# A graph network's edge pass on one core: other choice of column copies, a buffer of its own for the sums, and one-hot weights by whole-group operations

## The chip, the core and the metric

The kernel runs on one NeuronCore of a Trainium2 chip. Its engines are PE (TensorE: matmuls, with weight loads shown as PEld), DVE (VectorE), ACT (ScalarE), POOL (GpSimd) and SP (SyncE, which only issues transfers). The metric is the device time of one execution in microseconds (us), the median of several runs. Each engine has its own queue of instructions, works them off in order, and waits on semaphores for what other engines or transfers have to deliver.

## The reference

One layer of message passing over 12500 nodes (64 features) and 412500 directed edges, which are sorted by receiver and carry 32 features each. Cut to what matters:

```python
h = relu(layernorm(x))                                              # 12500 x 64
m = concat([h[senders], h[receivers], edge_features], -1)           # 412500 x 160
messages = silu(m @ W1 + b1) @ W2 + b2
att = softmax(silu(m @ Wa1 + ba1) @ Wa2 + ba2, axis=0)              # over ALL edges
aggregated = segment_sum(messages * att, receivers, 12500)
out = x + silu(concat([h, aggregated], -1) @ Wu1 + bu1) @ Wu2 + bu2
```

## The kernel before, in words

Edges are cut into 3224 tiles of 128 and those into 403 *groups* of 8 tiles (`K`). The input of both hidden layers is split: `h[senders] @ W` and `h[receivers] @ W` are computed once per node, not per edge.

**Node phase.** In chunks of up to 14 blocks of 128 nodes: layer norm, transposes into `hT` (128 partitions: even blocks in the lower 64, odd blocks in the upper 64), and from it two tables in DRAM of 128 columns a node: `ts_d` for senders (written from SP's queue) and `tr_d` for receivers (ACT's queue). A copy of `hT` goes to DRAM as `hT_d`.

**The loop over groups** (`one_pass`) emits its work in an order written out by hand; `pin` keeps it so in each engine's queue.

- `load(g + 2)`: POOL issues one indirect gather per tile (L533), 128 rows of `ts_d` by sender into the buffer `gs` (a pool of 7). Every fourth group, edge features and receivers' numbers come by SP. SP brings the window of receiver rows (L554). DVE builds the receivers' one-hot columns `eo` (L558), and PE adds window rows and edge features into `pe` (L562).
- `begin(g)`: DVE adds `pe` to the gathered rows, in place in `gs` (L573), ACT takes the tanh (L576).
- `end(g)`: DVE forms the messages (L586) and the attention logits (L592, L594, L597); a batch of 4 groups ends with its maximum (L609 to L616).
- `sum_up(done)`, some five groups behind: `weigh` updates the running maximum and takes exponentials; `by_node` makes the weights `wt`, the softmax weight times a one-hot of the receiver in a window of 40 nodes, by eight DVE operations, one per tile (L640), and PE sums the messages with them into `sp` (L646); `out_of` copies `sp` to `ss` on ACT (L652); `project` multiplies by W2 (L657); `put` adds to `sums` (L671, L675) and notes in `stand` which maximum the sums stand on (L678), for 64 partitions each.
- In a *chosen* group (127 of them) the eighth tile isn't gathered. ACT copies the senders' columns out of `hT` one by one (128 copies, L504, column numbers in registers), in bursts spread over three groups (`SLOTS`, two bursts a group). The column numbers are computed for each group on DVE (`places`, L487 to L493) from 128 copies of the sender list (`numbers`); another operation (L567) zeroes the half of the 128 partitions that isn't the sender's, and PE multiplies by `stack`, the weights laid over both halves.
- Between these, pieces of the last stage's inputs are made ahead (L348, L357, L389).

**The tail**, after the last group, makes 13 output tiles: `factor` (ACT, L830: exponential of the standing maximum less the last one), `first` (DVE L838, POOL L843), `silu` (ACT L848, DVE L849), `second` (PE L856), `rest` (DVE L862, transfers out). The loop of the tail issues, for tile number t, `first(t)`, `factor(t + 1)`, `silu(t - 1)`, `second(t - 1)`, `rest(t - 2)`.

`general` is another path for inputs whose receivers leave wide gaps; it isn't executed here.

Of the kernel before, what the change touches and what calls it, by code (L numbers as in the profile page):

```python
# [45 lines left out]
I32 = mybir.dt.int32  # L46
# [27 lines left out]
EVERY = 3  # L74
PHASE = 1
SLOTS = (((0, 24), (24, 24)), ((48, 24), (72, 12)), ((84, 24), (108, 20)))
# [4 lines left out]
BIG = 3.0e38  # L81


PARTS = [("pair", 4 * C), ("we", C), ("bias", C), ("wu2h", 2 * D), ("wa2", U), ("bu2", D), ("w_bu", U),
         ("w2b", U), ("wu1a", U), ("wu2", D), ("ba2", 1), ("w_bup", 2 * U), ("bu1", 1)]
# [5 lines left out]
def gnn_kernel(ctx: ExitStack, tc: tile.TileContext, n_edges, x, src, src_row, dst, dst_row, first, edge,  # L91
# [14 lines left out]
    hT_d = dram.tile([2 * D, NB // 2, P], F32, name="hT_d")  # L106
# [19 lines left out]
    w_bu = part["w_bu"][:D + 1]  # L126
# [29 lines left out]
    hT = const.tile([2 * D, NB // 2, P], F32, name="hT")  # L156
# [5 lines left out]
    gather = ctx.enter_context(tc.tile_pool(name="gather", bufs=7))  # L162


    with tc.tile_pool(name="node1", bufs=1) as node1, \
# [7 lines left out]
        for c, n in chunks:  # L173
            xc = node.tile([P, CB, D], F32, name="xc", bufs=min(len(chunks), 8))[:, :n, :]
# [138 lines left out]
        pin(nc.scalar.dma_start(hT_d, hT))  # L313
# [6 lines left out]


def node_bias(tc, b, v, work, ps):

    nc = tc.nc
    NB, w_bu = v["NB"], v["w_bu"]
    n = min(4, NB - b)
    hb = work.tile([D + 1, 4, P], F32, name="hb")
    nc.vector.memset(hb[D:, :, :], 1.0)
    for r in range(2):
        nc.sync.dma_start(hb[:D, r:n:2, :], v["hT_d"][r * D:(r + 1) * D, b // 2:(b + n) // 2, :])  # L330
    pb = ps.tile([P, 4, P], F32, name="mt")
    nc.tensor.matmul(pb[:U, :n, :], w_bu, hb[:, :n, :], start=True, stop=True)
    return pb[:U, :n, :]
# [60 lines left out]
def one_pass(tc, n_edges, v):  # L394
# [17 lines left out]
    with ExitStack() as ctx:  # L412
# [5 lines left out]
        stand = keep.tile([P, NH + 2 * W], F32, name="stand")  # L418
# [15 lines left out]
        nc.vector.memset(start[:, 1:2], BIG)  # L434
# [5 lines left out]
        hT = v["hT"].rearrange("d b p -> d (b p)")  # L440
        stack = keep.tile([2 * D, C], F32, name="stack")
        nc.vector.tensor_tensor(stack, v["w_pair"][:, 0, :C], v["w_pair"][:, 0, C:], ALU.add)
        half = keep.tile([P, 1], F32, name="half")
        nc.vector.memset(half[:D], 0.0)
        nc.vector.memset(half[D:], 1.0)
# [10 lines left out]
        with tc.tile_pool(name="work2", bufs=2) as work2, \  # L456
# [3 lines left out]
            pes, gss, lgs, ps_, psums, sps, pps, ees, mts, nums, cols = ({} for _ in range(11))  # L460
# [11 lines left out]
            chosen = {g for g in range(8, NG - 12) if g % EVERY == PHASE}  # L472

            def numbers(g):
                if g in chosen:
                    e = (g * K + K - 1) * EP
                    n = nums[g] = small.tile([P, EP], I32, name="num", bufs=2)
                    nc.sync.dma_start(n, bass.AP(tensor=v["src_row"].tensor,
                                                 offset=v["src_row"][:, e:].offset, ap=[[0, P], [1, EP]]))

            def places(g):
                if g not in chosen:
                    return
                n = nums[g]
                near = small.tile([1, EP], F32, name="near", bufs=1)
                to = small.tile([1, EP], I32, name="to", bufs=2)
                pin(nc.vector.tensor_scalar(to, n[0:1], 1, None, op0=ALU.logical_shift_right))  # L487
                m = NB // 2
                pin(nc.vector.tensor_scalar(near, to, 1.0 / m, 0.5 / m - 0.5, op0=ALU.mult, op1=ALU.add))
                pin(nc.vector.tensor_scalar(near, near, ROUND, None, op0=ALU.add))  # L490
                pin(nc.vector.tensor_scalar(near, near, ROUND, float(1 - m * P), op0=ALU.subtract, op1=ALU.mult))
                pin(nc.vector.scalar_tensor_tensor(to, to, float(P), near, op0=ALU.mult, op1=ALU.add))
                pin(nc.vector.tensor_scalar(n, n, 1, None, op0=ALU.bitwise_and))  # L493
                cols[g] = small.tile([P, EP], F32, name="cols", bufs=2), to

            def columns(g, first, n):
                if g not in chosen:
                    return
                to, at = cols[g]
                _, regs = nc.values_load_multi_w_load_instructions(  # L500
                    at[0:1, first:first + n], engines=[ENG.Activation], min_val=0, max_val=NP // 2 - 1,
                    skip_runtime_bounds_check_because=WHY)
                for i in range(n):
                    pin(nc.scalar.copy(to[:, first + i:first + i + 1], hT[:, bass.ds(regs[i], 1)]))  # L504
# [19 lines left out]
            def load(g):  # L524
# [40 lines left out]
                if g in chosen:  # L565
                    to, _ = cols[g]
                    pin(nc.vector.scalar_tensor_tensor(to, nums[g], half, to, op0=ALU.is_equal, op1=ALU.mult))  # L567
                    pin(nc.tensor.matmul(pe[:, K - 1, :], to, stack, start=False, stop=True))

            def begin(g):  # L570

                n = K - (g in chosen)
                pin(nc.vector.tensor_tensor(gss[g][:, :n, :], pes[g][:, :n, :], gss[g][:, :n, :], ALU.add))  # L573
                if n < K:
                    pin(nc.vector.tensor_copy(gss[g][:, n, :], pes[g][:, n, :]))
                pin(nc.scalar.activation(pes[g], gss[g], AF.Tanh))  # L576

            def end(g, then=None):
# [4 lines left out]
                gs, th = gss.pop(g), pes.pop(g)  # L583
# [50 lines left out]
            def by_node(g):  # L634
# [4 lines left out]
                for j in range(K):  # L639
                    pin(nc.vector.tensor_scalar(wt[:, j, :], iota_w[:EP, j // H, :],  # L640
                                                dloc[:, g * K + j:g * K + j + 1],
                                                p[:, k + j:k + j + 1],
                                                op0=ALU.is_equal, op1=ALU.mult))
# [5 lines left out]
            def out_of(g):  # L649
                sp = sps[g]  # L650
                ss = sps[g] = work2.tile([S1, W], F32, name="ss")
                pin(nc.scalar.copy(ss, sp))  # L652
# [7 lines left out]
            def put(g, part=None):  # L660
# [5 lines left out]
                for h, at in enumerate((at_lo, at_hi)):  # L666
                    rows, cols = slice(h * U, (h + 1) * U), bass.ds(at[g], W)
                    if part != "stand":
                        pp = pps[g]
                        if g == starts[s]:  # L670
                            pin(nc.vector.scalar_tensor_tensor(sums[rows, cols], sums[rows, cols],  # L671
                                                               scale[rows, s:s + 1], pp[rows],
                                                               op0=ALU.mult, op1=ALU.add))
                        else:
                            pin(nc.vector.tensor_tensor(sums[rows, cols], sums[rows, cols], pp[rows],  # L675
                                                        ALU.add))
# [11 lines left out]
            def inputs(t):  # L688

                n = P // 2 * NC  # L690
                if t < 8:
                    i = (t // 4 + (NG - 1) // NQ + 1) % 2
                    bs[t], xs[t] = eos[i][:, t % 4 * n:(t % 4 + 1) * n], hT[:, t * n:(t + 1) * n]
# [40 lines left out]

            for g in range(AHEAD):
                load(g)
            done = 0
            for g in range(NG):
# [9 lines left out]
                if g < 4:  # L748
                    w = -(-(NH + 2 * W) // 4)
                    for k, table in enumerate((sums, stand)):  # L750
                        piece = table[:, g * w:min((g + 1) * w, NH + 2 * W)]
                        pin(nc.scalar.activation(
                            piece, start[:, k:k + 1].to_broadcast([P, piece.shape[1]]), AF.Copy))
# [5 lines left out]
                numbers(g + 7)  # L759
                places(g + 6)  # L760
# [56 lines left out]
            free = [gather.tile([P, K, C], F32, name="gs").rearrange("p k c -> p (k c)") for _ in range(2)]  # L817
            free.append(hT[:, 8 * P // 2 * NC:8 * P // 2 * NC + K * C])
# [6 lines left out]
            def factor(t):  # L825
                n = width(t)
                if t in (1, 2):
                    acts_ps.append(one_ps.tile([P, 4, P], F32, name=(None, "sp", "mt")[t]).rearrange("p k c -> p (k c)"))
                fac = facs[t] = acts_ps[t % 3][:, :P // 2 * n]
                pin(nc.scalar.activation(fac.rearrange("u (p b) -> u p b", b=n),  # L830
                                         fv[:, :, t * NC:t * NC + n], AF.Exp, bias=last, scale=-1.0))
# [59 lines left out]
def general(tc, n_edges, v, dst):  # L891
# [7 lines left out]
    with ExitStack() as ctx:  # L899
# [11 lines left out]
        dst_sb = keep.tile([EP, T], I32, name="dst_g")  # L911
# [14 lines left out]
        with tc.tile_pool(name="bu_g", bufs=2) as work, \  # L926
                tc.tile_pool(name="bu_g_ps", bufs=2, space=PSUM) as bu_ps:
            for b in range(0, NB, 4):
                n = min(4, NB - b)
                bu = work.tile([U, 4, P], F32, name="bu_g")[:, :n, :]  # L930
                nc.scalar.copy(bu, node_bias(tc, b, v, work, bu_ps))
                nc.sync.dma_start(bu_d[:, b:b + n, :], bu)
# [142 lines left out]
def _laid_out(w):  # L1075
# [17 lines left out]
    part["w_bu"][:D + 1] = np.concatenate([w["Wu1"][:D], w["bu1"][None]])  # L1093
# [47 lines left out]
```

## Time and profile before

| | |
|---|---|
| median of 3 runs | 3987.03 us (3986.22 to 3988.06) |
| profiled execution | 3986.92 us, of it 3985.1 in the profile's span |
| busy: DVE / POOL / PE / ACT | 82% / 74% / 59% / 55% of the span |
| gathers (L533) | 3097, mean 947 ns |
| column copies (L504) | 16256 (127 groups x 128) |
| one-hot weights (L640) | 3224 operations, 726.1 us |
| mean clock granted to PE | 0.64 of full speed |

A row of the page's groups reads: line, engine, operation, out<-in, count, then busy us and mean ns of one, then the idle time of the engine just before these instructions and what ended most of it ("<-DMA gs": a transfer into `gs`; "<-issue": nothing the profile shows). A row of the timeline reads: start in us, length, engine, line, operation, and in brackets the idle time before it and who ended it.

### The profile page before, as it was taken

To read this page: it belongs to the slowest core of one execution; us is meant where nothing else is said; L and a number is where in the kernel's file an instruction comes from. 1 tells how busy PE (TensorE), PEld (TensorE's weight loads), DVE (VectorE), ACT (ScalarE), POOL (GpSimd) and SP (SyncE) were. 2 spreads that over 40 slices of the span, in tenths; PEclk is the share of its full clock that TensorE was granted. 3 is DMA by queue.
4 is the path that set the end of the run, shared out by engine and by line. 5 is a ranking of instruction groups with operands and counts; after the bars stand their busy time and mean duration, and the time that the engine had idled before them with its cause. 6 is when DMAs were issued, how large, how long until landed. Compare 5 with 4: busy or idle time off the path is not lost. (4 is left out here: it accounts for less than half of the span.)

```text
span 3985.1 us, 80416 instructions
## 1 busy us (share of the span) xinstructions
PE 2332.9 (59%) x11238; PEld 1888.3 (47%) x11238; DVE 3264.8 (82%) x9553; ACT 2173.0 (55%) x17477; POOL 2950.2 (74%) x3122
## 2 busy tenths in 40 slices
PE   6556566666666555555555555555655555555566
PEld 5444444454444444444444444444544444444455
DVE  6888888888888787888878888887878887878787
ACT  3655555555555555555555555555555555555512
POOL 3777777777777777777777777777777777777774
PEclk8766666666666666666666666666666665666666
DMA  8333343333333333333333333333333333333333
GB/s 287 101 99 99 95 110 92 103 99 102 102 92 95 93 85 93 87 92 88 89 94 84 95 93 86 94 84 94 88 91 94 84 95 87 91 95 84 104 105 85
DMA packets 219778, 391.64 MB, mean 98 GB/s; under 512 B 72209, under 2 KB 146898, under 8 KB 206050
## 3 DMA queue, kind: packets, MB, share of 16 engines
q0 software_dynamic: 99104, 203.16, 19.1%
q1 hardware_dynamic: 118754, 173.60, 16.7%
q10 hardware_dynamic: 1376, 9.67, 0.6%
q14 instruction: 452, 3.70, 0.3%
q8 instruction: 92, 1.51, 0.2%
HBM read 360.42 MB, written 25.72 MB: 97 GB/s over the span
## 5 line engine op out<-in xcount | busy, mean ns | idle before, releaser
L533 POOL DMA_INDIRECT gs<-ts_d,src_sb x3097 | 2933.0, 947 | 992.6 <-issue 854.1
L562 PE MATMUL pe<-wins,eo 128*128 128x256 f32 x3224 | 1465.1, 630 | 925.7 <-DVE eo L558 679.6
L504 ACT COPY cols<-hT 128x1 f32 x16256 | 1605.0, 187 | 717.7 <-issue 714.8
L562 PEld LDWEIGHTS pe<-wins,eo 128*128 128x128 f32 x3224 | 970.9, 318 | 1222.7 <-DVE eo L558 769.0
L576 ACT ACTIVATE pe<-gs 128x1024 f32<-128x1024 f32 x403 | 413.7, 1026 | 928.6 <-DVE gs L573 496.8
L573 DVE TENSOR_TENSOR gs<-pe,gs 128x1024 f32<-128x1024 f32 (+1 forms) x403 | 475.4, 1180 | 393.6 <-DMA gs<-ts_d,src_sb 369.2
L640 DVE TENSOR_SCALAR wt<-iota_w,dloc,p 128x40 f32<-128x40 f32 x3224 | 726.1, 321 | 1.8
L646 PE MATMUL sp<-wt,acts 128*65 128x40 f32 x6448 | 628.8, 268 | 6.3 <-DVE wt L640 3.9
L646 PEld LDWEIGHTS sp<-wt,acts 128*65 128x65 f32 x6448 | 589.9, 183 | 16.2 <-DVE wt L640 9.7
L657 PEld LDWEIGHTS mt<-ss,w2u 65*128 65x128 f32 x806 | 203.0, 279 | 336.2 <-issue 173.9
L657 PE MATMUL mt<-ss,w2u 65*128 65x40 f32 x806 | 181.6, 319 | 242.3 <-DVE gm L623 202.0
L616 PE MATMUL mt<-ident,mx 128*128 128x128 f32 x107 | 47.4, 443 | 445.8 <-DVE sums L675 427.2
L594 DVE TENSOR_TENSOR pe<-pe,w_all 128x512 f32<-128x512 f32 x403 | 281.8, 699 | 13.4
L558 DVE TENSOR_SCALAR eo<-dbs,bj 64x256 f32<-64x256 int32 x806 | 277.9, 375 | 18.2 <-DMA dbs<-in_dst_row_dram 9.0
L592 DVE SCALAR_TENSOR_TENSOR pe<-pe,gs 128x512 f32<-128x512 f32 x403 | 280.3, 696 | 10.5
L586 DVE SCALAR_TENSOR_TENSOR acts<-pe,gs 128x512 f32<-128x512 f32 x403 | 277.2, 688 | 12.4 <-ACT pe L576 3.2
L597 DVE TENSOR_REDUCE lg<-pe 128x8 f32<-128x512 f32 x403 | 277.0, 687 | 10.5
L616 PEld LDWEIGHTS mt<-ident,mx 128*128 128x128 f32 x107 | 19.5, 182 | 456.9 <-issue 455.0
L678 DVE COPY stand<-nmax 64x40 f32 x806 | 161.0, 200 | 3.2
L671 DVE SCALAR_TENSOR_TENSOR sums<-sums,scale,mt 64x40 f32 x214 | 54.2, 253 | 89.2 <-PE mt L657 85.0
L675 DVE TENSOR_TENSOR sums<-sums,mt 64x40 f32 x592 | 111.5, 188 | 4.7 <-PE mt L657 0.6
L357 DVE TENSOR_SCALAR bu<-mt,w_all 64x256 f32<-64x256 f32 (+1 forms) x50 | 23.9, 477 | 88.7 <-PE mt L348 88.3
(124 smaller groups left out, 1062.7 us busy)
## 6 DMA issues: line engine op xcount, KB each, us to landing
eo<-in_edge_dram SPq DMA_DIRECT2D x100, 512.0 KB
dbs<-in_dst_row_dram SPq DMA_DIRECT2D x200, 256.0 KB
gs<-ts_d,src_sb POOLq DMA_INDIRECT x3097
wins<-tr_d SPq DMA_DIRECT2D x806, 32.0 KB
num<-in_src_row_dram SPq DMA_DIRECT2D x127, 64.0 KB
ts_d<-ts SPq DMA_DIRECT2D x5, 896.0 KB
tr_d<-tr ACTq DMA_DIRECT2D x5, 896.0 KB
hT_d<-hT ACTq DMA_DIRECT2D x1, 3136.0 KB
```

The source lines that it names most:

```text
L504: pin(nc.scalar.copy(to[:, first + i:first + i + 1], hT[:, bass.ds(regs[i], 1)]))
L533: nc.gpsimd.indirect_dma_start(out=full[:rows, j, :], out_offset=None, in_=ts_d[:, :], in_offset=bass.IndirectOffsetOnAxis(ap=src_full[:ro ...
L558: pin(nc.vector.tensor_scalar(eo[:WR, e], db[:, e], bj[g // NQ % 2 * WR:(g // NQ % 2 + 1) * WR, g, h:h + 1], None, op0=ALU.is_equal))
L562: pin(nc.tensor.matmul(pe[:, 2 * q:2 * q + 2, :], eo[:, q * EP:(q + 1) * EP], win[:, q // 2, :, :], start=True, stop=q < H - 1 or g not in ...
L573: pin(nc.vector.tensor_tensor(gss[g][:, :n, :], pes[g][:, :n, :], gss[g][:, :n, :], ALU.add))
L576: pin(nc.scalar.activation(pes[g], gss[g], AF.Tanh))
L586: pin(nc.vector.scalar_tensor_tensor(acts[g % ACTS][:, :, 0:U], th[:, :, U:C], 1.0, gs[:, :, U:C], op0=ALU.add, op1=ALU.mult))
L592: pin(nc.vector.scalar_tensor_tensor(att, th[:, :, 0:U], 1.0, gs[:, :, 0:U], op0=ALU.add, op1=ALU.mult))
L594: pin(nc.vector.tensor_tensor(att, att, wa2[:EP, None, :].to_broadcast([EP, K, U]), ALU.mult))
L640: pin(nc.vector.tensor_scalar(wt[:, j, :], iota_w[:EP, j // H, :], dloc[:, g * K + j:g * K + j + 1], p[:, k + j:k + j + 1], op0=ALU.is_equ ...
L646: pin(nc.tensor.matmul(sp, acts[g % ACTS][:, j, :], wt[:, j, :], start=j == 0, stop=j == K - 1))
L657: pin(nc.tensor.matmul(pp, w2u.rearrange("s h u -> s (h u)"), sps.pop(g), start=True, stop=True))
```

## The change

It does five things together.

1. *Another choice of groups.* Chosen are now the groups from 10 to 390 whose number leaves 0 or 3 by five: 153, not 127. A chosen group's 128 copies come in five pieces of 28, 24, 28, 24 and 24, one per half step of the loop.
2. *Lists made once.* The column numbers of all chosen groups are computed at the start by 14 DVE operations and written to DRAM (`list_d`); each chosen group then loads its own 512 bytes (`listed`). The transposed nodes lie in a wider tile, `hS`, whose lower 64 partitions get a copy of the upper half (`upper`, four transfers on SP in the first four steps), so that a column is 64 partitions high, and the zeroing (L567) and `stack` are gone. `hT_d` and its write are gone. The upper 64 partitions of the added part of `hS` now hold `stand`, with 32 partitions per half in place of 64.
3. *A buffer of their own for the sums.* The addition writes to `sm` (2 buffers) and frees the gather's buffer, of which there are 5 in place of 7.
4. *Whole-group weights.* `by_node` has two operations over 128x320 (compare, multiply) in place of eight over 128x40. `out_of` copies on DVE in place of ACT.
5. *The tail.* Because `stand` has fewer partitions, `factor` first spreads its rows by a PE matmul with `pick` into PSUM, and ACT takes the exponential there. Two of the tail's spare buffers are taken from `sm`.

The diff, cut to its core ("..." marks what is left out):

```diff
-EVERY = 3
-PHASE = 1
-SLOTS = (((0, 24), (24, 24)), ((48, 24), (72, 12)), ((84, 24), (108, 20)))
+EVERY = 5
+LEADS = {0: 9, 3: 10}
+SLOTS = ((0, 28), (28, 24), (52, 28), (80, 24), (104, 24))
+FIRST = 10
...
-    hT_d = dram.tile([2 * D, NB // 2, P], F32, name="hT_d")
+    list_d = dram.tile([len(LEADS), P, EP], I32, name="list_d")
...
-    hT = const.tile([2 * D, NB // 2, P], F32, name="hT")
+    hS = const.tile([2 * D, NP + 2 * W], F32, name="hS")
+    hT = hS[:, :NP // 2].rearrange("d (b p) -> d b p", p=P)
...
-    gather = ctx.enter_context(tc.tile_pool(name="gather", bufs=7))
+    gather = ctx.enter_context(tc.tile_pool(name="gather", bufs=5))
...
-        pin(nc.scalar.dma_start(hT_d, hT))
...
-        stand = keep.tile([P, NH + 2 * W], F32, name="stand")
+        stand = v["hS"][D:, NH:]
...
-        stack = keep.tile([2 * D, C], F32, name="stack")
...
+        w_s = v["w_pair"][:D, 0, :C]
+        pick = keep.tile([P, P], F32, name="pick")
+        nc.vector.memset(pick, 0.0)
+        for h in range(2):
+            nc.vector.memset(pick[D + R * h:D + R * h + 1, h * U:(h + 1) * U], 1.0)
...
-            chosen = {g for g in range(8, NG - 12) if g % EVERY == PHASE}
+            chosen = [g for g in range(FIRST, NG - 12) if g % EVERY in LEADS]
+            def column_lists():
...
+                    pin(nc.vector.tensor_scalar(to, num, 1, None, op0=ALU.logical_shift_right))
...
+                    pin(nc.vector.scalar_tensor_tensor(column, num, float(NH), near, op0=ALU.mult, op1=ALU.add))
+                    nc.sync.dma_start(v["list_d"][i, :n, :], column)
+            def upper(k, n):
+                w = -(-NH // n)
+                a, b = k * w, min((k + 1) * w, NH)
+                nc.sync.dma_start(hS[:D, NH + a:NH + b], hS[D:, a:b])
+            def listed(g):
                 if g in chosen:
+                    to = lists[g] = small.tile([1, EP], I32, name="listed", bufs=3)
+                    nc.sync.dma_start(to, v["list_d"][list(LEADS).index(g % EVERY),
+                                                      (g - of_phase[g % EVERY][0]) // EVERY][None, :])
...
-                    pin(nc.scalar.copy(to[:, first + i:first + i + 1], hT[:, bass.ds(regs[i], 1)]))
+                    pin(nc.scalar.copy(cols[g][:, first + i:first + i + 1], hS[:D, bass.ds(regs[i], 1)]))
             def burst(g, k):
-                for i in range(EVERY):
-                    columns(g + 3 + i, *SLOTS[EVERY - 1 - i][k])
+                for c in range(g, g + 7):
+                    if c in chosen and 0 <= 2 * g + k - (2 * c - LEADS[c % EVERY]) < len(SLOTS):
+                        columns(c, *SLOTS[2 * g + k - (2 * c - LEADS[c % EVERY])])
...
-                    pin(nc.vector.scalar_tensor_tensor(to, nums[g], half, to, op0=ALU.is_equal, op1=ALU.mult))
-                    pin(nc.tensor.matmul(pe[:, K - 1, :], to, stack, start=False, stop=True))
+                    pin(nc.tensor.matmul(pe[:, K - 1, :], cols.pop(g), w_s, start=False, stop=True))
             def begin(g):
-                n = K - (g in chosen)
-                pin(nc.vector.tensor_tensor(gss[g][:, :n, :], pes[g][:, :n, :], gss[g][:, :n, :], ALU.add))
+                n, gs = K - (g in chosen), gss.pop(g)
+                sm = sms[g] = work2.tile([EP, K, C], F32, name="sm", bufs=2)
+                pin(nc.vector.tensor_tensor(sm[:, :n, :], pes[g][:, :n, :], gs[:, :n, :], ALU.add))
...
                 wt = work2.tile([EP, K, W], F32, name="wt")
                 p = ps_[batch[g]]
-                for j in range(K):
-                    pin(nc.vector.tensor_scalar(wt[:, j, :], iota_w[:EP, j // H, :],
-                                                dloc[:, g * K + j:g * K + j + 1],
-                                                p[:, k + j:k + j + 1],
-                                                op0=ALU.is_equal, op1=ALU.mult))
+                at = dloc[:, g * K:(g + 1) * K].rearrange("p (h j) -> p h j", h=2)
+                pin(nc.vector.tensor_tensor(wt.rearrange("p (h j) w -> p h j w", h=2),
+                                            iota_w[:EP, :, None, :].to_broadcast([EP, 2, H, W]),
+                                            at[:, :, :, None].to_broadcast([EP, 2, H, W]), ALU.is_equal))
+                pin(nc.vector.tensor_tensor(wt, wt, p[:, k:k + K, None].to_broadcast([EP, K, W]), ALU.mult))
...
-                pin(nc.scalar.copy(ss, sp))
+                pin(nc.vector.tensor_copy(ss, sp))
...
-                        pin(nc.vector.tensor_copy(stand[rows, cols],
-                                                  nmax[rows, s + 1:s + 2].to_broadcast([U, W])))
+                        pin(nc.vector.tensor_copy(stand[h * R:(h + 1) * R, cells],
+                                                  nmax[h * R:(h + 1) * R, s + 1:s + 2].to_broadcast([R, W])))
...
+            column_lists()
             for g in range(AHEAD):
                 load(g)
...
+                    upper(g, 4)
...
-                numbers(g + 7)
-                places(g + 6)
+                listed(g + 7)
...
-            free = [gather.tile([P, K, C], F32, name="gs").rearrange("p k c -> p (k c)") for _ in range(2)]
+            free = [work2.tile([P, K, C], F32, name="sm", bufs=2).rearrange("p k c -> p (k c)") for _ in range(2)]
...
-                pin(nc.scalar.activation(fac.rearrange("u (p b) -> u p b", b=n),
-                                         fv[:, :, t * NC:t * NC + n], AF.Exp, bias=last, scale=-1.0))
+                pin(nc.tensor.matmul(fac.rearrange("u (p b) -> u p b", b=n), pick[D:],
+                                     fv[:, :, t * NC:t * NC + n], start=True, stop=True))
+                pin(nc.scalar.activation(fac, fac, AF.Exp, bias=last, scale=-1.0))
```

More of the change, by code (lines that the diff above doesn't have):

```diff
@@ L319, in gnn_kernel @@
         general(tc, n_edges, locals(), dst[:EP])
[L322 to L333, printed above, removed]
 def tile_bias(tc, c, first, v, work, ps, bus):
@@ L459, in one_pass @@
                 tc.tile_pool(name="one_ps", bufs=1, space=PSUM) as one_ps:
-            pes, gss, lgs, ps_, psums, sps, pps, ees, mts, nums, cols = ({} for _ in range(11))
+            pes, gss, lgs, ps_, psums, sps, pps, ees, mts, lists, cols, sms = ({} for _ in range(12))
             w2t_ps = one_ps.tile([P, 4, P], F32, name="mt")[:U, 0, :S1]
@@ L481, in places @@
[L481 to L494, printed above, removed]
+            chosen = [g for g in range(FIRST, NG - 12) if g % EVERY in LEADS]
@@ L496, in columns @@
             def columns(g, first, n):
-                if g not in chosen:
-                    return
-                to, at = cols[g]
+                if first == 0:
+                    cols[g] = small.tile([D, EP], F32, name="cols", bufs=2)
                 _, regs = nc.values_load_multi_w_load_instructions(
-                    at[0:1, first:first + n], engines=[ENG.Activation], min_val=0, max_val=NP // 2 - 1,
+                    lists[g][0:1, first:first + n], engines=[ENG.Activation], min_val=0, max_val=NP - 1,
@@ L666, in put @@
                 for h, at in enumerate((at_lo, at_hi)):
-                    rows, cols = slice(h * U, (h + 1) * U), bass.ds(at[g], W)
+                    rows, cells = slice(h * U, (h + 1) * U), bass.ds(at[g], W)
                     if part != "stand":
```

86 lines of the change are left out of this document (52 added, 34 removed).

## The prediction

> **What bounds the kernel now.** I read the page's busy times and groups first, then the gathers' own line (mean/median/longest ns, first and last start), then POOL's waits (us, count, mean), one stretch of the timeline, and the tail last. The gathers on GpSimd (POOL) are the clock of the whole loop:
>
> ```profile
> span 3985.1 us, 80416 instructions
> PE 2332.9 (59%) x11238; PEld 1888.3 (47%) x11238; DVE 3264.8 (82%) x9553; ACT 2173.0 (55%) x17477; POOL 2950.2 (74%) x3122
> ...
> L533 POOL DMA_INDIRECT gs<-ts_d,src_sb x3097 | 2933.0, 947 | 992.6 <-issue 854.1
> L573 DVE TENSOR_TENSOR gs<-pe,gs 128x1024 f32<-128x1024 f32 (+1 forms) x403 | 475.4, 1180 | 393.6 <-DMA gs<-ts_d,src_sb 369.2
> L504 ACT COPY cols<-hT 128x1 f32 x16256 | 1605.0, 187 | 717.7 <-issue 714.8
> L640 DVE TENSOR_SCALAR wt<-iota_w,dloc,p 128x40 f32<-128x40 f32 x3224 | 726.1, 321 | 1.8
> ```
> ```profile
> L533 POOL DMA_INDIRECT gs<-ts_d,src_sb x3097: 940/944/1422, 49.8 to 3927.0; - x194
> ```
> ```profile
> POOL gs L533 <- issue: 854.1, 2802, 0.3
> POOL gs L533 <- DMA ts_d<-ts: 47.4, 1, 47.4
> ```
>
> POOL waits once, 47.4 us, for the table of sender rows, and after that only its own 0.3 us between gathers. The first of 3097 gathers starts at 49.8 and the last at 3927.0, so one costs (3927.0 - 49.8) / 3096 = 1.2523 us, 9.57 us per group of edges. VectorE (DVE), though busier in total, waits 369 us for gathers in L573. So the time is 49.8 of lead, 3877.2 of gathers, and 3985.1 - 3927.0 = 58.1 of tail. The profiled execution took 3986.92, 1.8 over its span and 0.1 under the median of 3987.03: the sum is made against it.
>
> The loop in close-up (start, length, engine):
>
> ```profile
> 2018.01 1.03 ACT L576 ACTIVATE pe<-gs 128x1024 f32<-128x1024 f32 x1 [2.06 <-DMA gs<-ts_d,src_sb]
> 2020.99 1.96 PE L646 MATMUL sp<-wt,acts 128*65 128x40 f32 x16
> 2023.25 0.94 POOL L533 DMA_INDIRECT gs<-ts_d,src_sb  x1 [0.30 <-issue]
> 2023.78 2.32 ACT L504 COPY cols<-hT 128x1 f32 x24 [1.46 <-issue]
> 2025.93 1.23 DVE L573 TENSOR_TENSOR gs<-pe,gs 128x1024 f32<-128x1024 f32 x1 [2.23 <-DMA gs<-ts_d,src_sb]
> 2028.24 0.94 POOL L533 DMA_INDIRECT gs<-ts_d,src_sb  x1 [0.31 <-issue]
> 2028.34 1.78 DVE L640 TENSOR_SCALAR wt<-iota_w,dloc,p 128x40 f32<-128x40 f32 x8
> 2029.49 0.94 POOL L533 DMA_INDIRECT gs<-ts_d,src_sb  x1 [0.30 <-issue]
> 2030.15 0.69 DVE L586 SCALAR_TENSOR_TENSOR acts<-pe,gs 128x512 f32<-128x512 f32 x1
> ```
>
> The addition of a group starts 2.68 us after its last gather does (2023.25 to 2025.93), when the rows have landed.
>
> **The change, part by part.**
>
> *Fewer gathers.* A chosen group gathers seven tiles, not eight. Before, 127 groups are chosen; after, numbers 10 to 390 that leave 0 or 3 by five, 77 + 76 = 153. 26 gathers go: 26 x 1.2523 = **-32.6**.
>
> *More column copies on ScalarE (ACT), and `ss` off it.* The groups of ACT and of DVE that this part and the next two use:
>
> ```profile
> L652 ACT COPY ss<-sp 65x40 f32<-65x40 f32 x395 | 71.9, 182 | 3.4 <-PE sp L646 3.4
> ```
> ```profile
> L489 DVE TENSOR_SCALAR near<-to 1x128 f32<-1x128 int32 x127 | 31.4, 247 | 4.3
> L609 DVE TENSOR_TENSOR lg<-lg,w_all 128x32 f32<-128x32 f32 x98 | 19.4, 198 | 3.3
> ```
>
> 26 x 128 copies more. Here ACT's cover counts: from the tanh at 2018.01 to the end of its second burst at 2026.10 are 8.09 us with 48 copies. After, every group has two bursts, 51.2 copies on average, at 2.32 / 24 = 0.097 each, and the copy of `ss` (0.18) goes to DVE: 8.09 + 0.31 - 0.18 = 8.2, some 8.4 with the exponentials of a batch. A group of 7.6 gathers lasts 9.5. Cost nothing, cover 1.1 us a group; without it, 403 x every us over.
>
> *DVE.* Per group the eight operations of L640 (726.1 / 403 = 1.80) become two over 128x320. By L389 (0.68 for 512 columns, below) and L609 (0.198 for 32), 320 columns are 0.49, two about 1.0. The copy of `ss` adds under 0.2, and the number arithmetic and `cols` mask go. DVE was busy 3264.8 / 403 = 8.1 a group and comes to about 7: off the path, cost and gain nothing by itself. The new wait of DVE for `sp` has PE's work behind it, over by 2022.95 (2020.99 + 1.96) for an addition at 2025.93: nothing.
>
> *What DVE does to the gathers.* This is the part that the busy times hide. L389 reads both inputs from SBUF, as the two new operations do (timeline: start, length):
>
> ```profile
> 498.48 0.68 DVE L389 TENSOR_TENSOR xt<-xt,w_all 128x512 f32<-128x512 f32 x1
> 498.55 1.42 POOL L533 DMA_INDIRECT gs<-ts_d,src_sb  x1 [0.30 <-DVE mx L614]
> 880.55 0.68 DVE L389 TENSOR_TENSOR xt<-xt,w_all 128x512 f32<-128x512 f32 x1
> 880.85 1.20 POOL L533 DMA_INDIRECT gs<-ts_d,src_sb  x1 [0.30 <-issue]
> ```
> A gather that starts inside such an operation is stretched to its end less 0.13: 499.16 - 498.55 - 0.13 = 0.48 (1.42 for 0.94), and 881.23 - 880.85 - 0.12 = 0.26. An operation of 0.49 can stretch one by at most about 0.33 and hits only starts in its first 0.36. Does it hit? DVE starts from the landing, so its place against the gathers is nearly fixed: L640 began at 2028.34, 0.10 behind a gather. With 0.1 for `ss` ahead, the pair runs 2028.44 to 2028.93 and 2028.96 to 2029.45; the next gather starts at 2029.49. Clear, but only 0.2 from a hit on either side, and the landing varies by about that. Bounds: 0; at random 2 x 0.36 / 1.25 x 0.17 = 0.1 a group, about 35; always the worst, 0.33 x 403 = 133. I take a fifth of random, nearest to the rows: **+7**. The other way, the eight short operations of L640 stretch gathers a little today: mean 947 against median 944, 3071 x 3 ns = 9 at most, 0 at least; I take **-8**.
>
> In the Trainium skill, "SBUF — State Buffer", section "Who interferes with whom", a DVE instruction with two SBUF inputs contends with a GpSimd instruction that reads SBUF, while `tensor_scalar` in its two-port mode locks GpSimd out altogether. The 1.42 and 1.20 agree with the first; for the second the trace shows only those 3 ns a gather. By the second alone the sum would lose its +7 and read 3977; by the first at random places it is the rival of 4012 below.
>
> *Gather buffers.* 7 become 5, but are freed by the addition instead of the group's end. Needed: the addition five groups back, some 40 us earlier. In the start-up it is nearest: group 5's gathers begin at 49.8 + 40 x 1.25 = 99.8, and the first addition ends at 95.8 below. Nothing; 4 us of cover.
>
> *Start-up.* The busy time of PE, PEld, DVE, ACT and POOL in a window (then clock, DMA share, GB/s), two lines of the timeline, one DMA issue:
>
> ```profile
> 40.00:50.00 10.00, 9.90 (x48) 8.41 (x48) 9.72 (x14) 4.08 (x9) 0.18 (x1) 1.00 0.66 265
> ```
> ```profile
> 88.86 1.28 DVE L558 TENSOR_SCALAR eo<-dbs,bj 64x256 f32<-64x256 int32 x4 [9.01 <-DMA dbs<-in_dst_row_dram]
> 94.58 1.23 DVE L573 TENSOR_TENSOR gs<-pe,gs 128x1024 f32<-128x1024 f32 x1 [4.44 <-PE pe L562]
> ```
> ```profile
> hT_d<-hT ACTq DMA_DIRECT2D x1, 3136.0 KB
> ```
>
> The four copies of the upper table (0.4 MB each) stand among the `ts_d` writes in SP's queue, three ahead of the last; the DMA engines are busy 0.66 there. 1.2 MB at 265 GB/s is 4.5 us at most, 0 if the idle third takes it: **+1**. The 14 list operations on DVE (L489's 0.25 each, 3.5 us) fit its 9.01 us wait at 88.86, and the 3.1 MB of `hT_d` no longer delay the loads there. The list's write waits on SP behind them, ahead of the second `dbs` load: hidden. Per-group loads of 64 KB become 0.5 KB on SP: nothing.
>
> *The tail.* `stand` keeps one row per half, so each of 13 output tiles needs a PE matmul of 512 columns (`pick`) before its exponential. The timeline at the end, and two windows:
>
> ```profile
> 3948.70 0.60 ACT L848 ACTIVATE pe<-gs 128x512 f32<-128x512 f32 x1 [1.71 <-POOL gs L843]
> 3949.34 0.69 DVE L849 SCALAR_TENSOR_TENSOR gs<-pe,gs 128x512 f32<-128x512 f32 x1 [1.37 <-ACT pe L848]
> 3950.08 3.91 PEld L856 LDWEIGHTS pe<-w_all,gs 128*128 128x128 f32 x16 [4.61 <-DVE gs L849]
> 3956.62 0.69 ACT L830 ACTIVATE pe<-stand,nmax 128x512 f32<-128x512 f32 x1 [0.76 <-DVE gs L849]
> 3957.25 0.59 ACT L848 ACTIVATE sp<-gs 128x512 f32<-128x512 f32 x1
> 3974.06 2.13 PE L856 MATMUL pe<-w_all,hT 128*128 128x128 f32 x8
> ```
> ```profile
> 50.00:60.00 10.00, 10.00 (x48) 8.82 (x47) 7.41 (x14) 0.00 (x0) 7.56 (x9) 1.00 0.88 332
> 3955.00:3960.00 5.00, 4.98 (x20) 4.59 (x21) 4.66 (x11) 3.10 (x6) 2.77 (x3) 0.68 0.57 135
> ```
>
> Today a tile takes (3974.06 - 3950.08) / 11 = 2.18 us. After, the queues close a ring: PE runs `second(t-1)`, then `pick(t+2)`; ACT runs `exp(t+2)` and only then `tanh(t)`; DVE's step on it releases `second(t)`. So per tile: `second` 3.91 / 2 = 1.95; `pick`, two passes of 512 columns. At full clock 48 passes of 256 columns took 10.00, 0.208 each, so 0.83, at the tail's 0.68 about 1.2, with 0.2 to drain 1.4; exponential to tanh 0.63 (3956.62 to 3957.25); tanh to DVE 0.64; DVE to PE 0.74. Together 5.3. Nine tiles at + 3.1 and one with a small `pick` at + 2.1 are 30; one `pick` ahead of the first tile adds 1.5, shorter weights in the last groups take 1 to 2 off: **+30**. Bounds: if only PE's own time counted, 10 x 0.8 = 8; with the half clock 36.
>
> Sum: -32.6 + 7 - 8 + 1 + 30 = -2.6, 3984.3 for the execution, **3984** as a median. 0.2% (8 us) is about what a measurement tells from no change.
>
> **The rivals.**
> - *The tail's ring does not close* (the steps overlap): then +8 there, -32.6 + 7 - 8 + 1 + 8 = -25, 3962. For it: PE idles for none of it today; against it: the fixed order in each queue.
> - *The weights hit the gathers.* This is the page's first rule as a mechanism here: the two-input pair lies 0.2 later or earlier than I place it. At random places 35 instead of 7: 4012; in every group, up to 4110. It decides (slower by over 8) from 0.05 us per group. For it: 1.42 and 1.20; against: the gap at 2029.45.
> - *ACT becomes the bound.* If its 8.4 were 9.6, 403 x 0.1 = 40 more: 4024. It decides from 9.53. Against: 1.1 us of cover.
>
> **How the numbers follow.** Sum as it stands 0.56, itself 3972 to 3998 (stretches 0 to 14, tail 24 to 36); ring open 0.15; weights hitting 0.21; ACT bound 0.08. Faster by over 0.2%: 0.15 + 0.15 from the low end of the first = 0.30. Slower: 0.19 + 0.08 + 0.06 = 0.33; the rest, 0.37, within. The range, 3963 to 4013, reaches to the open ring and to random hits.
>
> **What would show it.** The gathers: 3071, last start near 49.8 + 1 + 3070 x 1.252 = 3894. Weights: the longest and mean gather; a mean over 0.97 says they hit. Tail: last gather to end about 88 instead of 58, with PE, ACT and DVE taking turns. ACT: L573's wait for gathers should grow, since DVE is lighter; if it shrinks and tanh waits for no one, ACT bounds. Wrong if the tail is near 66, or if gathers are no longer 1.25 apart.

## The result and the profile after

The changed kernel takes 4038.44 us (median of 4 runs, 4033.63 to 4042.22) against 3987.55 for the kernel before: ratio 1.0127, 95% interval 1.011 to 1.0145. It is slower by 51 us, where 3984 was predicted; 4013 was the end of the range. The profiled execution took 4041.78, of it 4040.0 in the profile's span.

The page of the changed kernel (span, busy times, groups with busy us, mean ns | idle before):

```profile
span 4040.0 us, 82379 instructions
PE 2423.3 (60%) x11316; PEld 1899.1 (47%) x11316; DVE 2847.4 (70%) x6689; ACT 2411.4 (60%) x20402; POOL 2966.5 (73%) x3096
...
L537 POOL DMA_INDIRECT gs<-ts_d,src_sb x3071 | 2949.4, 960 | 985.4 <-issue 880.9
...
L579 ACT ACTIVATE pe<-sm 128x1024 f32<-128x1024 f32 x403 | 411.1, 1020 | 550.4 <-DVE ss L655 264.9
L576 DVE TENSOR_TENSOR sm<-pe,gs 128x1024 f32<-128x1024 f32 (+1 forms) x403 | 471.5, 1170 | 365.1 <-DMA gs<-ts_d,src_sb 347.9
...
L646 DVE TENSOR_TENSOR wt<-wt,p 128x320 f32<-128x320 f32 x403 | 198.3, 492 | 13.8
...
L643 DVE TENSOR_TENSOR wt<-iota_w,dloc 128x320 f32<-128x320 f32 x403 | 196.4, 487 | 3.7
```

The gathers' own line (shortest/median/longest ns, first and last start):

```profile
L537 POOL DMA_INDIRECT gs<-ts_d,src_sb x3071: 940/944/1604, 52.1 to 3936.3; - x192
```

The span can be taken apart as in the prediction. The lead grew from 49.8 to 52.1 (+2.3), the tail from 58.1 to 4040.0 - 3936.3 = 103.7 (+45.6). Between them 26 gathers went: 26 x 1.249 = -32.5, where 1.249 us is a gather of 0.944 with the usual 0.305 of idle time ahead of it. But the others got longer: the median is still 944 ns, and 3071 x 0.944 = 2899.0, so 2949.4 holds 50.4 us of *stretch*; before it was 2933.0 - 3097 x 0.944 = 9.4. That is +41.0. One wait of POOL of 1.8 us in the kernel before, by the profile for a gather's transfer, has nothing like it here, where the longest of these waits is the usual 0.3 (-1.5). Together 2.3 - 32.5 + 41.0 - 1.5 + 45.6 = 54.9 = 4040.0 - 3985.1.

```profile
POOL gs L533 <- DMA gs<-ts_d,src_sb: 46.9, 149, 1.8
```
```profile
POOL gs L537 <- DMA gs<-ts_d,src_sb: 63.4, 208, 0.3
```

What stretches a gather is seen in the timeline (start, length), at two places:

```profile
364.75 0.49 DVE L646 TENSOR_TENSOR wt<-wt,p 128x320 f32<-128x320 f32 x1
364.81 1.25 POOL L537 DMA_INDIRECT gs<-ts_d,src_sb  x1 [0.30 <-issue]
```
```profile
610.61 0.60 DVE L562 TENSOR_SCALAR eo<-dbs,bj 64x256 f32<-64x256 int32 x2
610.71 1.33 POOL L537 DMA_INDIRECT gs<-ts_d,src_sb  x1 [0.30 <-issue]
611.14 0.47 DVE L643 TENSOR_TENSOR wt<-iota_w,dloc 128x320 f32<-128x320 f32 x1
```

The first gather ends 0.82 after L646 does (366.06 and 365.24): it waits for the end of the operation inside which it started. The second starts inside the first of two L562 and ends 0.83 after the second of them (612.04 and 611.21).

Counted over all gathers of the trace, 300 start inside L643 or L646, and 203 of them are longer, by 29.0 us together. Of the 205 that start neither in the first 0.04 us of the operation nor in its last 0.14, 201 are longer; of the other 95, 2. Of the 320 that start inside L576, which is longer than both but has one of its inputs in PSUM, 1 is longer.

215 gathers start inside L562, and 96 of them are longer, by 18.0 us together. Before, 18 that started inside that operation (there L558) were, by 1.7. L562 reads one tensor and one number per partition. It goes with the operation behind: of 135 gathers inside an L562 whose next operation starts before it has ended, 95 are longer; of 80 where the next one starts later, 1 is. Why that is so stays open.

The tail, one tile of it in the timeline, then a window of it in this kernel and one in the kernel before (PE, PEld, DVE, ACT, POOL, clock, DMA share, GB/s):

```profile
3970.12 2.07 PE L835 MATMUL sp<-hS,pick 64*128 64x512 f32 x2
3972.23 0.66 ACT L837 ACTIVATE sp<-sp,nmax 128x512 f32<-128x512 f32 x1 [5.06 <-PE sp L835]
3972.81 0.59 ACT L854 ACTIVATE mt<-hS 128x512 f32<-128x512 f32 x1
3973.44 0.69 DVE L855 SCALAR_TENSOR_TENSOR hS<-mt,hS 128x512 f32<-128x512 f32 x1 [4.16 <-ACT mt L854]
3974.18 2.24 PE L862 MATMUL pe<-w_all,hS 128*128 128x128 f32 x8 [1.99 <-DVE hS L855]
3976.35 2.07 PE L835 MATMUL mt<-hS,pick 64*128 64x512 f32 x2
```
```profile
3950.00:4040.00 90.00, 54.27 (x144) 33.07 (x144) 29.16 (x68) 14.76 (x26) 15.61 (x13) 0.50 0.15 37
```
```profile
3945.00:3985.00 40.00, 26.31 (x100) 24.01 (x100) 26.91 (x57) 14.56 (x24) 15.66 (x13) 0.67 0.35 83
```

Each of the ring's steps starts when the one before it ends, 6.23 us a tile (3970.12 to 3976.35), and the granted clock is 0.50, where it was 0.67.

### The profile page after: what moved, and what is told of

Same layout as the page of the kernel before. It is cut to its first block, busy times and chain, and to the rows that moved or that the text cites. A ratio compares the mean times of both kernels' runs of the same rounds, so it can differ in the third digit from the quotient of the medians.

```text
span 4040.0 us, 82379 instructions
## 1 busy us (share of the span) xinstructions
PE 2423.3 (60%) x11316; PEld 1899.1 (47%) x11316; DVE 2847.4 (70%) x6689; ACT 2411.4 (60%) x20402; POOL 2966.5 (73%) x3096
## 5 line engine op out<-in xcount | busy, mean ns | idle before, releaser
L537 POOL DMA_INDIRECT gs<-ts_d,src_sb x3071 | 2949.4, 960 | 985.4 <-issue 880.9
L507 ACT COPY cols<-hS 64x1 f32 x19584 | 1919.1, 187 | 899.6 <-issue 838.7
L566 PE MATMUL pe<-wins,eo 128*128 128x256 f32 x3224 | 1475.4, 637 | 1108.6 <-issue 549.3
L566 PEld LDWEIGHTS pe<-wins,eo 128*128 128x128 f32 x3224 | 1004.6, 326 | 1381.0 <-issue 630.1
L579 ACT ACTIVATE pe<-sm 128x1024 f32<-128x1024 f32 x403 | 411.1, 1020 | 550.4 <-DVE ss L655 264.9
L576 DVE TENSOR_TENSOR sm<-pe,gs 128x1024 f32<-128x1024 f32 (+1 forms) x403 | 471.5, 1170 | 365.1 <-DMA gs<-ts_d,src_sb 347.9
L649 PE MATMUL sp<-wt,acts 128*65 128x40 f32 x6448 | 602.9, 265 | 24.0 <-DVE wt L646 24.0
L589 DVE SCALAR_TENSOR_TENSOR acts<-pe,sm 128x512 f32<-128x512 f32 x403 | 278.4, 691 | 168.3 <-ACT pe L579 159.4
L595 DVE SCALAR_TENSOR_TENSOR pe<-pe,sm 128x512 f32<-128x512 f32 x403 | 281.9, 700 | 13.6
L562 DVE TENSOR_SCALAR eo<-dbs,bj 64x256 f32<-64x256 int32 x806 | 271.1, 374 | 8.0
L646 DVE TENSOR_TENSOR wt<-wt,p 128x320 f32<-128x320 f32 x403 | 198.3, 492 | 13.8
L643 DVE TENSOR_TENSOR wt<-iota_w,dloc 128x320 f32<-128x320 f32 x403 | 196.4, 487 | 3.7
L681 DVE COPY hS<-nmax 32x40 f32 x806 | 163.4, 203 | 13.9 <-issue 0.3
```

Of the source, the lines that this page charges most:

```text
L507: pin(nc.scalar.copy(cols[g][:, first + i:first + i + 1], hS[:D, bass.ds(regs[i], 1)]))
L537: nc.gpsimd.indirect_dma_start(out=full[:rows, j, :], out_offset=None, in_=ts_d[:, :], in_offset=bass.IndirectOffsetOnAxis(ap=src_full[:ro ...
L562: pin(nc.vector.tensor_scalar(eo[:WR, e], db[:, e], bj[g // NQ % 2 * WR:(g // NQ % 2 + 1) * WR, g, h:h + 1], None, op0=ALU.is_equal))
L566: pin(nc.tensor.matmul(pe[:, 2 * q:2 * q + 2, :], eo[:, q * EP:(q + 1) * EP], win[:, q // 2, :, :], start=True, stop=q < H - 1 or g not in ...
L576: pin(nc.vector.tensor_tensor(sm[:, :n, :], pes[g][:, :n, :], gs[:, :n, :], ALU.add))
L579: pin(nc.scalar.activation(pes[g], sm, AF.Tanh))
```

## The experiments

Two theories. **P**: a gather that starts inside a VectorE operation with two inputs in SBUF is held until it ends (L562 is not covered by these words, but in the changed kernel such an operation, L643, is queued behind it); **ring**: the tail waits in a circle through PE, ACT and VectorE. Against P stands B, that another part of the change holds the gathers; against the ring C, that the tail is merely slow.

### Four kernels on another chip

*Eight weight operations again* in the changed kernel (the loop of L640 for the two operations):

> The changed kernel with the eight one-tile weight operations of before (compare and multiply in one, a scalar per row) in place of the two whole-group ones; all else as changed. Theory P (a gather that starts inside a VectorE operation with two inputs in SBUF is held until that operation ends): the two operations and the receiver one-hots queued right ahead of them hold about 47 of the 51 us by which gathers exceed their usual spacing; these go, the excess falls to 10 to 15 us as in the kernel before, and the time to 3996 to 4006. Rival B (the gathers are held by what else changed: five buffers, the copy of ss on VectorE, other transfers): excess and time stay, 4034 to 4042.

*One input in PSUM* (cut to its core):

```diff
+                bank = banks.pop(g) if g in banks else with_iota(g)   # ScalarE: bank[:, 3, :2*W] = iota_w
+                iota_ps = bank[:, 3, :2 * W].rearrange("p (h w) -> p h w", h=2)
+                same = bank[:EP].rearrange("p a b -> p (a b)")[:, 64:64 + K * W]
-    tensor_tensor(wt, iota_w, at, is_equal);  tensor_tensor(wt, wt, p, mult)
+    tensor_tensor(same, iota_ps, at, is_equal);  tensor_tensor(wt, same, p, mult)
```

> The changed kernel, its two whole-group weight operations kept in size and number, but each with one of its two inputs in PSUM (the window numbers are copied there by ScalarE once a group, the comparison's result goes there). Theory P: with one SBUF input the gathers are not held; excess below 15 us, time 3995 to 4006, the operations themselves no shorter than 0.48. Rival W (any long VectorE operation that reads broadcast operands or writes the 128x320 tile holds them): excess about 50 and 4034 to 4042.

*The kernel before with the two whole-group operations alone*:

> The kernel before with the two whole-group weight operations alone; all else as before. Theory P: the starts of gathers fall evenly over the operations, so the excess over the usual spacing rises from 11 us to 40 to 55 and the time from 3987 to 4016 to 4031. Prediction's own term (the operations' place in the group keeps clear of the gathers): 3980 to 3988. Rival B (what holds the gathers is another part of the change): 3985 to 3989.

*The tail in another order* (the order of issue, cut to its core):

```diff
-   first(t); factor(t + 1)                    ; silu(t - 1)                    ; second(t - 1)
+   first(t); pick(t + 1)                      ; silu(t - 1); exponential(t + 1); second(t - 1)
```

> The changed kernel with the tail's queue on ScalarE in another order: the tanh of tile t - 1 is issued ahead of the exponential of tile t + 1, all else as changed. Ring theory (pick, exponential, tanh, VectorE's step and second wait for each other in a circle, 6.23 us a tile): the circle opens, PE runs pick and second back to back, 2.07 + 2.24 = 4.3 to 4.5 us a tile, and the time falls by 18 to 22 us to 4016 to 4022. Rival C (the tail is as long as PE's slower clock makes it, whatever the order): within 3 us of 4038.

On this chip the kernel before took 5934.01 us. The four took 6301.79, 6350.98, 5828.86 and 6238.54, and no expectation of a time can be read. The first of them, POOL's and ACT's groups:

```profile
L537 POOL DMA_INDIRECT gs<-ts_d,src_sb x3071 | 2900.2, 944 | 3249.0 <-issue 926.4 <-DVE sm L578 871.2 <-DVE sm L576 689.2
```
```profile
L507 ACT COPY cols<-hS 64x1 f32 x19584 | 2200.1, 187 | 3152.4 <-issue 3106.5 <-PE mt L660 18.6 <-DMA dbs<-in_dst_row_dram 8.5
```

Ahead of its column copies ACT waits 3106 us for nothing that the profile shows (838.7 in the changed kernel's own profile), a copy itself is as long as ever, and POOL waits for VectorE's additions. Only the gathers' lengths can be read: the stretch is 1.2 us here (2900.2 - 2899.0), and 29.5 in the fourth run, which has the two whole-group operations (later expectations give 2.7 and 31.0, and 5.9 for the next run, counting the lengthened gathers alone):

```profile
L537 POOL DMA_INDIRECT gs<-ts_d,src_sb x3071 | 2928.5, 954 | 3195.8 <-issue 933.4 <-DVE sm L578 821.4 <-DVE sm L576 757.6
```

In the other two, the gathers inside the weight operations can be counted: with one input in PSUM 183 start inside them and none is longer; in the kernel before with the two whole-group operations 212 start inside and 72 are longer, by 9.8 us together.

### The same on a chip where the kernel before takes 3987

> The changed kernel with the eight one-tile weight operations of before, once more: on the chip of the first four runs the kernel before itself took 5934 us, with the engines waiting for their own instructions, so that those times could not be laid beside 3987 and 4038; of the gathers there only the lengths could be read (2.7 us of stretch with these weights, 31.0 with the two whole-group operations). Where the kernel before takes about 3987: theory P 3996 to 4006 with an excess of the gathers of 10 to 15 us; rival B 4034 to 4042.

4054.63, ratio 1.0169 (1.0152 to 1.0186). P's expectation of the time (3996 to 4006) failed. The stretch went, as P says, and further than the 10 to 15 us expected:

```profile
L537 POOL DMA_INDIRECT gs<-ts_d,src_sb x3071 | 2904.3, 946 | 1036.3 <-issue 911.0 <-DVE ss L655 28.6 <-DMA gs<-ts_d,src_sb 22.2
```

Stretch 5.3 (2904.3 - 2899.0), but idle time 1036.3 in place of 985.4: POOL now waits some 51 us, for the addition that frees its buffers: of its 21 waits over 0.6 us, 20 end 0.27 us after an L576 (the rows below name whichever VectorE operation ended last ahead of the gather). All these waits lie between 550 and 1250 us, most of them four groups apart. The waits there:

```profile
DVE bu L348 <- PE mt L339: 73.6, 17, 5.5
DVE sums L674 <- PE mt L660: 39.7, 17, 3.2
POOL gs L537 <- DVE ss L655: 28.3, 10, 4.3
POOL gs L537 <- DVE sm L578: 19.6, 7, 2.9
DVE sm L576 <- DMA gs<-ts_d,src_sb: 0.6, 3, 0.2
```

VectorE no longer waits for gathers (0.6), but 4.3 us at a time in L348 for a PE matmul queued behind those of L566. That is theory **Q**, tried below.

> The changed kernel, each of the two whole-group operations with one input in PSUM, once more for the same reason. Where the kernel before takes about 3987: theory P 3995 to 4006, excess of the gathers below 15 us; rival W (the whole-group form itself holds the gathers) 4034 to 4042. ScalarE's copy of the window numbers adds 0.2 us a group; its cover is about 1 us.

4029.57, ratio 1.0108 (1.0091 to 1.0125). The time is again above what P gave, and POOL's idle time is up by 36.9 us (1022.3 - 985.4): 19 waits over 0.6 us, all between 650 and 1250 us, 18 of them ending 0.27 us after an L576. VectorE also waits 256.6 us here for ScalarE's copy of the window numbers, so the two causes are not apart in this run.

```profile
L537 POOL DMA_INDIRECT gs<-ts_d,src_sb x3071 | 2902.0, 945 | 1022.3 <-issue 909.0 <-DVE ss L666 25.7 <-DMA gs<-ts_d,src_sb 23.8
```
```profile
L653 DVE TENSOR_TENSOR sp<-sp,dloc 128x320 f32<-128x320 f32 x403 | 201.7, 501 | 260.8 <-ACT sp L641 256.6
L656 DVE TENSOR_TENSOR wt<-sp,p 128x320 f32<-128x320 f32 x403 | 198.0, 491 | 13.7
```

The two operations are as long as before, yet the stretch is 3.0 (2902.0 - 2899.0): 311 gathers start inside them, and none is longer. So with these operations it is the second SBUF input, not their length or their number. In the Trainium skill, "SBUF — State Buffer", section "Who interferes with whom", two SBUF inputs contend with a GpSimd instruction that reads SBUF; these runs agree. For `tensor_scalar` in its two-port mode it states a full block; in `w8_again` the eight short ones stretched 47 of 591 gathers, by 29 ns on average, and whether they ran in that mode no run shows.

> The changed kernel with tanh of tile t - 1 ahead of the exponential of tile t + 1, once more. Ring theory: 4.3 to 4.5 us a tile in place of 6.23, time 4016 to 4022 where the kernel before takes 3987; rival C: within 3 us of 4038.

4015.16, ratio 1.007 (1.0053 to 1.0087), a little below the 4016 to 4022 expected. The ring opens:

```profile
3961.66 2.23 PE L864 MATMUL pe<-w_all,sm 128*128 128x128 f32 x8
3963.82 2.07 PE L835 MATMUL sp<-hS,pick 64*128 64x512 f32 x2
3965.83 2.23 PE L864 MATMUL pe<-w_all,hS 128*128 128x128 f32 x8
```

```profile
3955.00:4000.00 45.00, 44.34 (x112) 26.77 (x111) 24.48 (x46) 14.28 (x25) 15.49 (x13) 0.50 0.23 56
```

PE runs back to back, 4.17 us a tile (4.3 to 4.5 was expected), and the tail is 4015.4 - 3933.5 = 81.9. So 21.8 of the tail's 45.6 us lay in the order of ScalarE's queue; most of the rest is PE's own work, 4.17 us a tile against 2.18 in the kernel before.

*No pick at all*: in the last groups ScalarE lays the maxima over 128 partitions, and the exponential reads SBUF (cut to its core):

```diff
+   i, w = 2 * (g - 389) + k, -(-NH // 4)            # half steps of groups 389 to 394
+   rows, part = i // 4 * R, stand[R * (i // 8):R * (i // 8) + R]
+   nc.scalar.copy(hS[rows:rows + R, NH + a:NH + b], part[:, a:b])      # quarter i % 4
-   matmul(fac, pick, fv); activation(fac, fac, Exp)
+   activation(fac, hS[:, NH:], Exp)
```

> The changed kernel with the standing maxima laid over all 128 partitions again before the tail: in the last groups, where no columns are copied any more, ScalarE copies the two 32-row blocks four times over, in 12 pieces, into the part of the wide tile that the columns no longer need; the tail then has no pick matmul and takes its exponential from SBUF as before. Ring theory: with pick gone the tail falls back from 103.7 us to 58 to 64 and the time by 40 to 46 to 3992 to 3998 where the kernel before takes 3987. Rival C (the tail is long because of the other buffers it uses, or the clock): it stays above 80 us, time above 4015. If the pieces hold up the tanh of the last groups, some 5 us of the gain go.

```profile
L547 POOL DMA_INDIRECT gs<-ts_d,src_sb x3071: 940/944/1605, 51.5 to 3932.5; - x192
```

3996.50, ratio 1.0025 (1.0015 to 1.0035). The last gather starts at 3932.5 and the span is 3994.5: a tail of 62.0, 41.7 less. Time and tail are as the ring theory gave them, and C is out.

### The sum of the parts

> The kernel before with the two whole-group weight operations alone, once more, for a chip where the kernel before takes about 3987. Theory P: the excess of the gathers over their spacing rises from 11 us to 40 to 55, the time to 4012 to 4031; VectorE has 0.8 us a group less to do, which gives nothing, as POOL does not wait for it. Prediction's own term: 3980 to 3988.

4024.05, ratio 1.0088 (1.0071 to 1.0105). The stretch is 2971.5 - 3097 x 0.944 = 47.9, and time and stretch are as P gave them, so the weights alone do in the kernel before what they do in the changed one; B is out. Here, too, not all of it lies inside the two operations: 29.6 us do, and 10.8 fall on 23 gathers that start inside L493, the last of the column numbers' operations, which is queued right ahead of the weights.

```profile
L533 POOL DMA_INDIRECT gs<-ts_d,src_sb x3097 | 2971.5, 959 | 993.0 <-issue 873.8 <-DMA ts_d<-ts 48.2 <-DMA gs<-ts_d,src_sb 20.5
```

*Eight operations, bias pieces early*: `tile_bias(...)` is called ahead of `burst(g, 0)` and `load(g + AHEAD)`, not behind them.

> As the changed kernel with the eight weight operations (4054.6 us, gathers stretched by 5.9 us only, but 50.6 us of waits of POOL for its buffers, all between 550 and 1250 us, one every four groups), with the pieces of the next layer's bias (PE L339, VectorE L348) issued ahead of the loads of the next group, so that VectorE's step no longer waits 4.3 us behind the eight matmuls of L566. Theory Q (in groups 16 to 120 VectorE's queue with this wait in it is what ends last, once the gathers are not stretched): the waits of POOL fall below 15 us, time 4003 to 4020. Rival D (VectorE's 0.8 us more work a group, or ScalarE's column copies, set the pace there by themselves): POOL's waits stay above 35 us, 4040 to 4056.

4004.33, ratio 1.004 (1.0026 to 1.0054). Q holds: VectorE and ScalarE have as much work as in `w8_again`, and 50 us went with the order alone. D is out.

```profile
L537 POOL DMA_INDIRECT gs<-ts_d,src_sb x3071 | 2903.7, 946 | 985.8 <-issue 905.0 <-DMA gs<-ts_d,src_sb 24.4 <-DVE wt L643 17.1
```
```profile
L348 DVE TENSOR_SCALAR bu<-mt,w_all 64x256 f32<-64x256 f32 (+1 forms) x50 | 23.9, 478 | 28.7 <-PE mt L339 28.3
```

POOL's idle time is back at 985.8, from 1036.3; L348 waits 28.3 us in all, in place of 110.0 in `w8_again` and 111.3 in the changed kernel.

> The changed kernel with one input of each whole-group weight operation in PSUM (the window numbers are put there once, not once a group), and the bias pieces issued ahead of the loads. Theories P and Q together: no stretch (below 6 us), POOL's waits for buffers below 10 us, last gather at 3890 to 3900, the tail as in the changed kernel, time 3992 to 4004. If P or Q fails: above 4020.

```profile
L542 POOL DMA_INDIRECT gs<-ts_d,src_sb x3071: 940/945/1457, 51.7 to 3891.6; - x192
```

3999.23, ratio 1.0026 (1.0016 to 1.0036); time and last gather are as expected, with ScalarE's copy and the wait of L348 both out of the way. The stretch, 2905.3 - 2899.0 = 6.3, is just above the 6 expected (the median here is 945), and the tail is 106.0, 2.3 longer than in the changed kernel.

*All three*: PSUM weights, early bias pieces, spread maxima, and `upper` one group later.

> The same with the tail of the run with the maxima spread over 128 partitions, and the four copies of the upper table issued one group later, so that they stand behind the last write of the sender rows. Theories P, Q and the ring add up: first gather at 50 to 52, last at 3888 to 3898, tail 58 to 64, time 3950 to 3965, faster than both kernels. If they overlap: above 3975.

3963.31, ratio 0.9936 (0.9919 to 0.9953): faster than both kernels. Two figures missed.

```profile
L552 POOL DMA_INDIRECT gs<-ts_d,src_sb x3071: 940/945/1363, 54.6 to 3894.1; - x192
```
```profile
POOL gs L552 <- DMA hS<-hS: 52.2, 1, 52.2
```

The later copies did not help the start (54.6, not 50 to 52): by the profile the first gather's wait ended with one of them. The tail is 3962.7 - 3894.1 = 68.6, not 58 to 64: three tiles of `second` take 8.59 us here (3917.04 to 3925.63) and 6.56 in `tail_spread` (3954.90 to 3961.46). Two of the tail's three buffers are halves of one PSUM tile here, and I have not tried them apart.

## Why the prediction was wrong

- **Gathers, -32.6**: right. 3071 went out, 1.249 us apart without the stretch (1.265 with it); all_three keeps the gain.
- **Stretches, +7 - 8**: wrong, +41.0, and the first of two steps that failed. "DVE starts from the landing, so its place against the gathers is nearly fixed" was read from one group and then taken for 403. The starts fall evenly: (0.487 + 0.492) x 403 / 1.25 = 316 at random, 300 counted. The rival "at random" gave 35 and 4012, with a chance of 0.21 (its own terms, 2 x 0.36 / 1.25 x 0.17 x 403, come to 39, which is 4016); 29.0 was measured. The law behind it, a start held to the operation's end, was right. It left out L562, which holds gathers for 18.0 us in the changed kernel, and for 3.8 and 3.1 with the eight or the PSUM operations behind it. The sign "a mean over 0.97" was set too high: the mean rose only to 0.960, and 16 ns a gather are the 50 us. (In the gathers' own line the first number is the shortest, not the mean, as the prediction has it.)
- **Old stretches of L640, -8**: too large; the gathers that start inside L640 in the kernel before are longer by 3.2 us together, and with the eight operations kept in the changed kernel the whole stretch is 5.3.
- **Tail, +30**: the second step that failed. The mechanism was right, the term was too small: 45.6. Ten intervals of 6.23 - 2.18 are 40.5. In the ring `pick` costs 2.11, not 1.4 (3970.12 to 3972.23), and `second` 2.17, not 1.95 (3974.18 to 3976.35). `pick` was priced at a clock of 0.68, but 0.50 was granted: its 0.83 at full clock would then be 1.66, with the 0.2 some 1.9 as an estimate, which is most of the difference and not all. `second` was taken from half a row of weight loads (3.91); its matmuls took 2.13 in the kernel before already.
- **Start-up, +1**: +2.3, not explained further.
- **VectorE off the path, "cost and gain nothing by itself"**: right in the changed kernel, but only because stretched gathers were slower still. Its sign missed: the addition's wait for gathers did not grow but fell, from 369.2 to 347.9 us. The wait of L348 stood in the profile of before (there L357, waits between 550 and 1250 us), and I read VectorE's mean of 8.1 us a group instead of that stage:

```profile
DVE bu L357 <- PE mt L348: 58.7, 17, 4.5
```

- **ACT's cover, gather buffers**: right; ScalarE still idles 550.4 us ahead of the tanh (L579), for VectorE, and POOL waits for no buffer in the changed kernel.

## What to carry to other kernels

Where one engine issues at a fixed beat and another can hold it, count over all beats how often they meet before believing in a gap seen in one period. Here one input in PSUM was enough for an operation to hold no gather any more, at no cost in its length (501 and 491 ns against 487 and 492). And when a bottleneck is removed, look for the stage with the least cover, not at the mean: here the stretch hid a wait of VectorE in groups 16 to 120, and when the stretch was gone POOL idled 37 to 51 us more.

## What the hardware showed beyond that

One chip ran the kernel before in 5934 us, 1.49 times 3987. There engines idle for nothing that the profile shows: in the changed kernel with eight weight operations ACT does so for 3106.5 us ahead of the column copies. On that chip the two whole-group weights, 6 x 403 operations fewer, gained 1.7% (5828.86), where they cost 0.9% elsewhere. What slows that chip stays open. And PE's granted clock fell from 0.67 to 0.50 in the changed kernel's tail, in which PE was busy 60% of the time. Its waits alone do not explain it, for it was 0.50 as well in `tail_order_again`, where PE was busy for 44.34 of 45 us; what sets it stays open.
